# A graph-attention layer over sorted edges: 250 blocks of edges instead of 252

## The chip, the cores and the metric

The kernel runs on one core of one Trainium2 chip. The metric is the time of one launch on the device in microseconds (us). Several launches are timed and their median is given. One further launch was recorded by the hardware profiler, and everything that is read from a trace below comes from that single launch.

## The reference

There are N = 30000 nodes of 256 features and E = 510000 edges, one in each direction of 240000 random pairs and one loop for each node. The edges are sorted by their destination, and each has one of 8 types. The layer is

```
feat[r, n, h, :] = layernorm(x)[n] @ conv_weights[r, h]            # 8 types, 4 heads of 64
e[edge, h]  = leaky_relu(feat[type, src] . attn_l + feat[type, dst] . attn_r)
alpha       = softmax of e over the edges that share a destination
x           = x + sum over edges of alpha * feat[type, src] + h_bias
x           = x + (shared MLP + the two best of four expert MLPs)(layernorm(x))
```

A destination has about 17 edges. Which edges belong to which destination is only known from the data, so the kernel works it out on the chip.

## The kernel before

**Stage A** makes `feat` for all nodes. It runs over 235 tiles of 128 nodes. For each tile, TensorE makes five groups of columns (`group`, L304), ScalarE and VectorE bring them from PSUM into a tile `fo` (L306, L308), and SyncE stores the 1 MB of it to DRAM (`store`, L318). There are seven `fo` buffers. `erp_d` (what a destination contributes to the score) and `xb_d` (the input plus bias) are stored beside it.

While stage A runs, **side work** is slipped in. It is written as Python generators in a list `side`: `edge_records`, then `places`, then `expert_weights`. The function `aside` runs the first of them to its next `yield`. It is called once in a tile while `edge_records` is running, and twice in a tile afterwards (L699). So a `yield` more in `edge_records` puts off everything after it by one tile, and the order of instructions on each engine's queue is settled by that.

`edge_records` packs the edges into records, and then finds where the blocks begin. Edges are cut every `S` edges. Since a destination must not be split, block b begins at the first destination that begins at or after edge b*S. The block's first edge goes to `lo_sb`, its first node to `n_sb`. A block holds at most `CAP` = 2048 edges (16 for each of 128 partitions) and at most 128 nodes. The number of blocks is NBLK = ceil((E - CAP) / S), that is 252 with S = 2016, and one last block with 18 edges for each partition takes the end of the list. If a limit is broken, `bad` becomes 1, and a slow general path runs after the fast one (L1222 onward).

`places` runs over batches of 12 blocks: it loads their records (`fetch`, L519), prepares masks and indices on VectorE and GpSimd, and stores them to `rk_d` and `dk_d` (L590, L591). When all batches are done, two small tables go through TensorE and ScalarE to `thr_d` (L598, L601, L603).

`first_rows` starts when the tile counter m reaches `BT` + 2 = 178. For each block it gathers the `feat` rows of one edge for each partition (128 rows of 1040 bytes) with an indirect DMA on GpSimd (L632), and SyncE stores them to `stage` (L627). The gathers are spread evenly over the groups of the last 57 tiles.

**Stage B** runs over the blocks t = 0 .. NBLK. For a block, GpSimd gathers the other 15 rows for each partition with 15 indirect DMAs (`gather`, L962; the last block has 18), into a ring of four blocks. VectorE, ScalarE and TensorE make the scores, the softmax and the weighted sums (`dest_select`, `dest_pick`, `scores`, `weigh`, `onehot`, `sums`), each part emitted in one of six slots of a block. Blocks are put together in groups of four (`sizes`, L1127) for the MLPs: each group's 22 or so steps go into a list `todo`, and one step is taken in each slot.

The order of the work is written out by hand in both stages; no scheduler moves it.

Of the kernel before, what the change touches and what calls it, by code (L numbers as in the profile page):

```python
# [10 lines left out]
F32 = mybir.dt.float32  # L11
BF16 = mybir.dt.bfloat16
I32 = mybir.dt.int32
I16 = mybir.dt.int16
AF = mybir.ActivationFunctionType
ALU = mybir.AluOpType
AX = mybir.AxisListType
# [4 lines left out]
P = 128  # L22
# [9 lines left out]
EP = 120  # L32
EG = 85

U = 16
CAP = U * P
S = 2016
UL = 18  # L40
T = 4

# [3 lines left out]

WI, WD, WA, WP, W1 = 0, U, 2 * U, 3 * U, 5 * U
WT = W1 + 2 * (U + 1)
WR = WT + U * R // 2

# [6 lines left out]
def kernel(  # L57
# [26 lines left out]
    nc = tc.nc  # L84
    N = x.shape[0]
    E = src.shape[0]
# [4 lines left out]
    NGRP = EP * GPP  # L91
    NBLK = -(-(E - CAP) // S)
    NQ = NB
    assert EP * EG * GPP == E and 512 <= N < 32768 and NBLK * S + 64 <= E

    dram = ctx.enter_context(tc.tile_pool(name="dram", bufs=1, space=DRAM))
# [9 lines left out]
    thr_d = dram.tile([NBLK, 2, P], F32, name="thr_d")  # L106
    exc_d = dram.tile([P], F32, name="exc_d")
    KT = -(-(NBLK + 1) // P)
    lo_d = dram.tile([KT, P], F32, name="lo_d")
    n_d = dram.tile([KT, P], F32, name="n_d")  # L110
    uns_d = dram.tile([EP], F32, name="uns_d")
    mnmx = dram.tile([2, NGRP], F32, name="mnmx")
    lohi_d = dram.tile([NT, 2], I32, name="lohi_d")

# [19 lines left out]
    def layernorm(pool, xg, n, name, m=P):  # L134
# [10 lines left out]
        for t in range(n):  # L145
# [9 lines left out]
    w2 = wf.tile([P, 2, P], F32, name="w2")  # L155
# [15 lines left out]
                            pattern=[[1, NE], [-1, NE]], channel_multiplier=0)  # L171
# [10 lines left out]
                            pattern=[[1, P]], channel_multiplier=1)  # L182
# [38 lines left out]
    with ExitStack() as cx:  # L221
        wp = cx.enter_context(tc.tile_pool(name="wconv", bufs=1))
        xp = cx.enter_context(tc.tile_pool(name="xa", bufs=2))
        gp = cx.enter_context(tc.tile_pool(name="groups", bufs=1))
        cl = ExitStack()
# [119 lines left out]
        def edge_records(cl):  # L345
# [8 lines left out]
            n = gs * EG  # L354
            uns = gp.tile([EP, nch], F32, name="uns")
            ep = cl.enter_context(tc.tile_pool(name="edges", bufs=2))
            for c in range(nch):
# [8 lines left out]
                else:  # L366
                    nc.vector.memset(d_sb[:, 0:1], -1)
                    nc.sync.dma_start(d_sb[:, 1:], dstv[:, :n])
                    with nc.allow_non_contiguous_dma(reason="one edge of each partition, once"):
# [25 lines left out]
            zx = gp.tile([P, D], F32, name="zx")  # L395
# [6 lines left out]
                              zx.bitcast(BF16)[:, :R * 3 * H])  # L402
            yield


            WN = 64
            FAR = float(1 << 23)
            dw = gp.tile([P, KT, WN + 1], I32, name="dw")
            nc.gpsimd.memset(dw, -1)
            jj = gp.tile([P, WN], F32, name="jj")  # L410
            nc.gpsimd.iota(jj, pattern=[[1, WN]], base=0, channel_multiplier=0,
                           allow_small_or_imprecise_dtypes=True)
            first = gp.tile([P, KT], F32, name="first")
            irow = gp.tile([P, 1], F32, name="irow")
            nc.gpsimd.iota(irow, pattern=[[0, 1]], base=0, channel_multiplier=1,
                           allow_small_or_imprecise_dtypes=True)
            yield
            for k in range(KT):
                nc.vector.tensor_scalar(first[:, k:k + 1], irow, float(S), float(k * P * S), op0=ALU.mult,
                                        op1=ALU.add)  # L420
            nc.sync.dma_start(dw[0:1, 0, 1:], dst[0:WN].rearrange("(o c) -> o c", o=1))
            for k in range(KT):
                a = 1 if k == 0 else 0
                n = min(P, NBLK + 1 - k * P)
                nc.sync.dma_start(dw[a:n, k, :],
                                  bass.AP(tensor=dst.tensor, offset=dst.offset + (k * P + a) * S - 1,
                                          ap=[[S, n - a], [1, WN + 1]]))
            before_last = gp.tile([1, 1], I32, name="before_last")
            nc.sync.dma_start(before_last, dst[E - UL * P - 1:E - UL * P].rearrange("(o c) -> o c", o=1))
            yield  # L430
            lof = gp.tile([P, 2, KT], F32, name="lof")
            miss = gp.tile([P, KT, WN], F32, name="miss")
            nc.vector.tensor_tensor(miss, dw[:, :, 1:], dw[:, :, :WN], op=ALU.is_equal)
            yield
            for i, v in enumerate((jj[:, None, :].to_broadcast([P, KT, WN]), dw[:, :, 1:])):
                cand = gp.tile([P, KT, WN], F32, name="cand")
                nc.vector.scalar_tensor_tensor(cand, miss, FAR, v, op0=ALU.mult, op1=ALU.add)
                nc.vector.tensor_reduce(lof[:, i, :], cand, AX.X, ALU.min)
                yield
            nc.vector.tensor_add(lof[:, 0, :], lof[:, 0, :], first)  # L440
            nc.vector.tensor_scalar_min(lof[:, 0, :], lof[:, 0, :], float(E))
            nc.vector.tensor_scalar(lof[:, 1, :], lof[:, 1, :], 0.0, float(N), op0=ALU.max, op1=ALU.min)
            yield
            lor = gp.tile([1, KT * P], F32, name="lor")
            nr = gp.tile([1, KT * P], F32, name="nr")
            with nc.allow_non_contiguous_dma(reason="first edges and nodes of blocks, once"):
                for i, (t_d, row) in enumerate(((lo_d, lor), (n_d, nr))):
                    nc.sync.dma_start(t_d.rearrange("k p -> p k"), lof[:, i, :])
                    yield
                    if i:  # L450
                        nc.sync.dma_start(t_d[0:1, 0:1], zx[0:1, 0:1])
                        yield
                    nc.sync.dma_start(row, t_d.rearrange("(o k) p -> o (k p)", o=1))
                    yield
            nc.vector.tensor_copy(lo_sb, lor)
            nc.vector.tensor_copy(n_sb, nr)
            nc.vector.tensor_scalar_min(n0_sb, nr, float(N - P))
# [1 line left out]
            yield  # L459
            nc.vector.tensor_scalar(rowid[:, :NBLK], nbc, irow, None, op0=ALU.add)  # L460
            nc.vector.tensor_scalar_add(rowid[:, NBLK:], irow, float(N - P))
            unm = gp.tile([EP, 1], F32, name="unm")
            nc.vector.tensor_reduce(unm, uns, AX.X, ALU.max)
            yield
            with nc.allow_non_contiguous_dma(reason="one number of each partition, once"):
                nc.sync.dma_start(uns_d.rearrange("(p o) -> p o", o=1), unm)
            yield
            unr = gp.tile([1, EP], F32, name="unr")
            nc.sync.dma_start(unr, uns_d.rearrange("(o p) -> o p", o=1))


            two = gp.tile([1, 5], F32, name="two")
            gap = gp.tile([1, NBLK], F32, name="gap")
            for i, (row, most) in enumerate(((lor, CAP), (nr, P))):
                nc.vector.tensor_sub(gap, row[:, 1:NBLK + 1], row[:, :NBLK])
                nc.vector.tensor_reduce(two[:, i:i + 1], gap, AX.X, ALU.max)
# [4 lines left out]
            yield  # L481
            nc.vector.tensor_reduce(two[:, 4:5], unr, AX.X, ALU.max)
            nc.vector.tensor_reduce(bad, two, AX.X, ALU.max)

        BT = 3 * NT // 4
        count = {"ready": 0, "sent": 0}
# [3 lines left out]
        def places(cl):  # L490
# [3 lines left out]
            batches = [(b, min(GB, NBLK - b)) for b in range(0, NBLK, GB)]  # L494
            UW = U + 1
            no = gp.tile([1, 16], I16, name="no")
            nc.gpsimd.memset(no, -1)
            nc.sync.dma_start(dk_d[NBLK * CAP:].rearrange("(o c) -> o c", o=1), no)
            iu = gp.tile([P, U], F32, name="iu")
            nc.gpsimd.iota(iu, pattern=[[1, U]], base=0, channel_multiplier=0, allow_small_or_imprecise_dtypes=True)  # L500
# [142 lines left out]
        with tc.manual_schedule():  # L643
# [27 lines left out]
            while slot < 16:  # L671
                attention(slot, ab)
                slot += 1
            cl.close()
            side = [edge_records(cl), places(cl), expert_weights()]
            ahead = first_rows()

# [204 lines left out]
    with ExitStack() as cx:  # L882
# [242 lines left out]
        groups = {}  # L1125

        left, sizes = (NBLK + 1) % T, [T] * ((NBLK + 1) // T)  # L1127
        sizes = sizes[:-1] + [T - 1, 2] if left == 1 else sizes + [left] if left else sizes[:-1] + [2, 2]
        member = [(sum(sizes[:q]), n) for q, n in enumerate(sizes) for _ in range(n)]
        todo = []  # L1130
        late = []
# [91 lines left out]
    with tc.tile_pool(name="gr2", bufs=1) as gp, tc.tile_pool(name="ed2", bufs=2) as ep:  # L1223
        with tc.For_i(0, again):
# [4 lines left out]
            for g0 in range(0, GPP, gs):  # L1229
                c0, n = g0 * EG, gs * EG  # L1230
# [11 lines left out]
            base = gp.tile([P, ntg], F32, name="base")  # L1242
# [32 lines left out]
            for g in range(ntg):  # L1275
                n = min(P, NT - g * P)
# [3 lines left out]
    with ExitStack() as cx:  # L1280
# [13 lines left out]
        irow = cp.tile([P, 1], F32, name="irow")  # L1294
# [159 lines left out]
```

## Time and profile before

| | |
|---|---|
| median of 3 runs | 8487.05 us (8483.83 to 8509.22) |
| the profiled execution | 6603.28 us, of it the span 6601.5 us |
| mean granted TensorE clock in the span | 0.971 |
| stage A, first instruction to last matmul | 0 to about 1730 us |
| first gather of stage B, last one | 1750.3 us, 6513.1 us |
| busy, share of the span | PE 92%, DVE 80%, POOL 62%, ACT 52% |
| indirect gathers | 252 in stage A, 3798 in stage B |

PE is TensorE, DVE is VectorE, ACT is ScalarE, POOL is GpSimd, SPq is the queue of SyncE. The profiled execution is 22% shorter than the timed runs. The trace shows nothing of the difference, so it can be read only as to which engine waits for which, and by how much in that execution. The page gives, for each group of instructions, the number of them, their busy time, the mean duration of one, and the idle time of the engine ahead of them with what ended it. A window row gives a stretch of time, its length, the busy time (and count) of PE, PEld, DVE, ACT and POOL in it, the granted clock, the mean busy share of the 16 DMA engines and the GB/s they moved.

### The profile page before, as it was taken

To read this page: it belongs to the slowest core of one execution; us is meant where nothing else is said; L and a number is where in the kernel's file an instruction comes from. 1 tells how busy PE (TensorE), PEld (TensorE's weight loads), DVE (VectorE), ACT (ScalarE), POOL (GpSimd) and SP (SyncE) were. 2 spreads that over 40 slices of the span, in tenths; PEclk is the share of its full clock that TensorE was granted. 3 is DMA by queue.
4 is the path that set the end of the run, shared out by engine and by line. 5 is a ranking of instruction groups with operands and counts; after the bars stand their busy time and mean duration, and the time that the engine had idled before them with its cause. 6 is when DMAs were issued, how large, how long until landed. Compare 5 with 4: busy or idle time off the path is not lost. (4 is left out here: it accounts for less than half of the span.)

```text
span 6601.5 us, 97367 instructions
## 1 busy us (share of the span) xinstructions
PE 6047.9 (92%) x25770; PEld 3891.0 (59%) x25771; DVE 5254.8 (80%) x13699; ACT 3405.3 (52%) x8758; POOL 4082.8 (62%) x4424
## 2 busy tenths in 40 slices
PE   9999999999689989989899998899899999988998
PEld 5555555555356666666666666666666666666665
DVE  5555767644488888898888898898888888888895
ACT  2222222222256566666666665666656666566664
POOL 1111111266677777777777777777777777777773
PEclk9999999999899999999999999999999999999998
DMA  6666676799855555555555555555555555555552
GB/s 228 226 210 200 226 238 225 247 337 330 267 160 163 161 164 163 163 163 160 165 163 163 160 164 165 163 160 161 164 162 167 158 163 164 163 165 159 163 163 74
DMA packets 764586, 1214.72 MB, mean 184 GB/s; under 512 B 242498, under 2 KB 602917, under 8 KB 733813
## 3 DMA queue, kind: packets, MB, share of 16 engines
q1 hardware_dynamic: 568581, 668.72, 31.4%
q0 software_dynamic: 194400, 539.40, 29.3%
q8 instruction: 209, 3.42, 0.2%
q14 instruction: 356, 2.92, 0.1%
q10 hardware_dynamic: 1040, 0.26, 0.0%
HBM read 821.54 MB, written 386.43 MB: 183 GB/s over the span
## 5 line engine op out<-in xcount | busy, mean ns | idle before, releaser
L962 POOL DMA_INDIRECT ft<-feat,rk x3798 | 3606.7, 950 | 1169.0 <-issue 390.3
L1122 PE MATMUL po<-ft,oh 128*128 128x260 f32 x8100 | 2189.0, 407 | 137.1 <-DVE ho L1147 128.6
L1122 PEld LDWEIGHTS po<-ft,oh 128*128 128x128 f32 x8100 | 1520.4, 201 | 433.8 <-issue 196.5
L304 PE MATMUL ps<-w,xT 128*128 128x448 f32 (+1 forms) x4700 | 1708.4, 519 | 2.0 <-DMA w<-_L_gnn_conv_weights_dram 2.0
L1115 DVE TENSOR_TENSOR ft<-ft,p 128x768 f32<-128x768 f32 x1518 | 1292.2, 852 | 90.0 <-ACT ft L1108 86.1
L1049 ACT ACTIVATE oh<-icol,rk 128x128 f32<-128x128 f32 x4032 | 1327.7, 389 | 0.0
L304 PEld LDWEIGHTS ps<-w,xT 128*128 128x128 f32 x4700 | 875.6, 190 | 689.1 <-issue 603.3
L306 ACT COPY fo<-ps 128x448 f32<-128x448 f32 (+1 forms) x711 | 378.0, 533 | 1062.5 <-PE ps L304 972.5
L1050 ACT ACTIVATE oh<-oh 128x384 f32<-128x384 f32 x1518 | 741.1, 488 | 48.1
L1026 PEld LDWEIGHTS <-ohT 128*128 128x128 bf16 x4050 | 378.2, 158 | 408.9 <-issue 332.6
L1039 DVE TENSOR_REDUCE e<-ere 128x16 f32<-128x384 f32 (+1 forms) x1012 | 561.3, 555 | 34.6
L1037 DVE TENSOR_TENSOR ere<-pe,rk 128x384 f32<-128x384 f32 x1008 | 550.8, 546 | 1.3 <-PE pe L1026 1.3
L1107 ACT ACTIVATE p<-e 128x64 f32<-128x64 f32 (+1 forms) x253 | 70.2, 277 | 839.2 <-DVE e L1061 808.1
L1026 PE MATMUL pe<-erp,ohT 128*128 128x96 bf16 x4050 | 438.8, 233 | 60.5 <-DVE ohT L1009 37.5
L818 PE MATMUL ph<-xT,v 128*128 128x512 f32 (+2 forms) x1024 | 490.3, 602 | 0.4 <-ACT a L819 0.4
L306 DVE COPY fo<-ps 128x448 f32<-128x448 f32 (+1 forms) x464 | 242.3, 527 | 200.4 <-PE ps L304 194.1
L293 DVE COPY xT<-ptr 128x256 f32<-128x256 f32 x229 | 97.0, 424 | 368.6 <-PE ptr L291 367.0
L632 POOL DMA_INDIRECT fr<-feat,lowc x252 | 239.7, 951 | 193.7 <-DMA stage<-fr 90.2
L1009 DVE TENSOR_SCALAR ohT<-dr,rowid 128x2064 bf16<-128x2064 int16 (+1 forms) x253 | 323.6, 1279 | 19.8 <-DMA stage<-fr 19.7
L273 POOL TENSOR_TENSOR xb<-xg,hb 128x1024 f32<-128x1024 f32 (+1 forms) x59 | 140.7, 2385 | 272.1 <-DMA xg<-in_x_dram 161.9
L993 PE MATMUL t<-ident,fb 128*8 128x128 f32 x506 | 104.3, 290 | 214.9 <-DVE fb L1072 214.7
L819 ACT ACTIVATE a<-ph,c 128x512 f32<-128x512 f32 (+2 forms) x256 | 173.6, 678 | 195.7 <-PE ph L818 195.7
(219 smaller groups left out, 6810.9 us busy)
## 6 DMA issues: line engine op xcount, KB each, us to landing
feat<-fo SPq DMA_DIRECT2D x234, 1040.0 KB
dr<-dk_d SPq DMA_DIRECT2D x252, 516.0 KB
ft<-feat,rk POOLq DMA_INDIRECT x3798
stage<-fr SPq DMA_DIRECT2D x84, 390.0 KB
ft<-stage SPq DMA_DIRECT2D x252, 130.0 KB
xt<-xb_d SPq DMA_DIRECT2D x253, 128.0 KB
out_dram<-og SPq DMA_DIRECT2D x253, 128.0 KB
xb_d<-xb SPq DMA_DIRECT2D x58, 512.0 KB
```

The lines of the kernel that those rows point to most:

```text
L304: nc.tensor.matmul(ps, t["xT"][:, k, :], w[:, k, c0:c1], start=k == 0, stop=k == 1)
L306: eng(t["fo"][:, h0:h1, :HD], ps[:, :n].rearrange("p (a d) -> p a d", d=HD))
L818: nc.tensor.matmul(ps[:, :self.w], lhs, rhs, start=i == 0, stop=i == len(pairs) - 1)
L962: nc.gpsimd.indirect_dma_start(out=s.ft[:, u].rearrange("p h d -> p (h d)"), out_offset=None, in_=feat[:, :], in_offset=bass.IndirectOffse ...
L1009: nc.vector.tensor_scalar(ohT[:, :3 * s.dw].rearrange("n (i e) -> n i e", i=3), s.dr[:, :, :s.dw], rowid[:, t:t + 1], None, op0=ALU.is_equal)
L1026: nc.tensor.matmul(pe[:, u - u0].rearrange("p f r -> p (f r)"), s.ov[:, u, :], s.erp.rearrange("n h k r -> n (h k r)"), start=True, stop=True)
L1037: nc.vector.tensor_mul(ere, s.pe[:, :u1 - u0], s.th[:, u0:u1, None, :].to_broadcast([P, u1 - u0, H * 3, R]))
L1039: nc.vector.tensor_reduce(s.e[:, :, u0:u1].rearrange("p h u -> p u h"), ere.rearrange("p u (h k) r -> p u h (k r)", h=H), AX.X, ALU.add)
L1049: nc.scalar.activation(s.oh[:, u, :], icol, AF.Abs, bias=s.nd[:, u:u + 1])
L1050: nc.scalar.activation(s.oh[:, u0:u1], s.oh[:, u0:u1], AF.Relu, bias=1.0, scale=-1.0)
L1115: nc.vector.tensor_mul(fc, fc, pc[:, :, None].to_broadcast([P, (u1 - u0) * H, HD]))
L1122: nc.tensor.matmul(s.po.rearrange("n h d -> n (h d)"), s.oh[:, u, :], s.ft[:, u].rearrange("p h d -> p (h d)"), start=u == 0, stop=u == s. ...
```

## The change

`S` becomes 2032, so NBLK becomes ceil(507952 / 2032) = 250. The room for a border to slide falls from 32 edges to 16. Therefore each border now has two candidates: the destination that begins last before edge b*S, and the one that begins first at or after it. For each block it is worked out whether it keeps both limits if it begins early (`may[:, 0]`) and if it begins late (`may[:, 1]`), with its end at the late candidate. One scan over the borders then settles which candidate each takes: `late[b+1] = max(late[b] + may1 - 1, may0)`. The first edges and nodes are mixed from the candidates by `late`.

The window of edges looked at doubles from 64 to 128 for each border, four candidate rows go through DRAM (`cand_d`) into one partition instead of two rows, and the result `n_d` is stored from there. The small tiles of this part move from the pool `gp`, which lives for all of stage A, to a pool `bounds` that takes the place of the closed `edges` pool and is closed at the end of `edge_records`; `places` opens its own pool after it. The last lines let the MLP groups be cut for 251 blocks: one group of 2 in front, 61 of 4, then 3 and 2.

```diff
-S = 2016
+S = 2032
@@ edge_records
+            bp = cl.enter_context(tc.tile_pool(name="bounds", bufs=1))
-            dw = gp.tile([P, KT, WN + 1], I32, name="dw")
+            dw = bp.tile([P, KT, 2 * WN + 1], I32, name="dw")
...
-            for i, v in enumerate((jj[:, None, :].to_broadcast([P, KT, WN]), dw[:, :, 1:])):
-                cand = gp.tile([P, KT, WN], F32, name="cand")
-                nc.vector.scalar_tensor_tensor(cand, miss, FAR, v, op0=ALU.mult, op1=ALU.add)
-                nc.vector.tensor_reduce(lof[:, i, :], cand, AX.X, ALU.min)
-                yield
+            for i, v in enumerate((jj[:, None, :].to_broadcast([P, KT, 2 * WN]), dw[:, :, 1:])):
+                for f, (far, op) in enumerate(((-FAR, ALU.max), (FAR, ALU.min))):
+                    w2 = slice(f * WN, (f + 1) * WN)
+                    cand = bp.tile([P, KT, WN], F32, name="cand")
+                    nc.vector.scalar_tensor_tensor(cand, miss[:, :, w2], far, v[:, :, w2], op0=ALU.mult, op1=ALU.add)
+                    nc.vector.tensor_reduce(lof[:, i, f, :], cand, AX.X, op)
+                    yield
...
-                for i, (t_d, row) in enumerate(((lo_d, lor), (n_d, nr))):
-                    nc.sync.dma_start(t_d.rearrange("k p -> p k"), lof[:, i, :])
-                    yield
-                    if i:
-                        nc.sync.dma_start(t_d[0:1, 0:1], zx[0:1, 0:1])
-                        yield
-                    nc.sync.dma_start(row, t_d.rearrange("(o k) p -> o (k p)", o=1))
-                    yield
+                for k in range(4):
+                    nc.sync.dma_start(cand_d[k].rearrange("k p -> p k"), lof[:, k // 2, k % 2, :])
+                    yield
+                yield
+                nc.sync.dma_start(cands.rearrange("o i k -> o (i k)"),
+                                  cand_d.rearrange("(o i) k p -> o (i k p)", o=1))
+                yield
+                yield
+            nc.vector.memset(cands[:, 2:, 0:1], 0.0)
+            may = bp.tile([1, 2, NBLK], F32, name="may")
+            for f in range(2):
+                for i, most in enumerate((CAP, P)):
+                    gap = bp.tile([1, NBLK], F32, name="gap")
+                    nc.vector.tensor_sub(gap, cands[:, 2 * i + 1, 1:NBLK + 1], cands[:, 2 * i + f, :NBLK])
+                    if i == 0:
+                        nc.vector.tensor_scalar(may[:, f], gap, float(most), None, op0=ALU.is_le)
+                    else:
+                        nc.vector.scalar_tensor_tensor(may[:, f], gap, float(most), may[:, f], op0=ALU.is_le,
+                                                       op1=ALU.mult)
+                yield
+            nc.vector.tensor_scalar_add(may[:, 1], may[:, 1], -1.0)
+            late = bp.tile([1, KT * P], F32, name="late")
+            nc.vector.memset(late, 1.0)
+            nc.vector.tensor_tensor_scan(late[:, 1:NBLK + 1], may[:, 1], may[:, 0], 1.0, ALU.add, ALU.max)
+            yield
+            for i, row in enumerate((lor, nr)):
+                nc.vector.tensor_sub(row, cands[:, 2 * i + 1], cands[:, 2 * i])
+                nc.vector.tensor_mul(row, row, late)
+                nc.vector.tensor_add(row, row, cands[:, 2 * i])
+                yield
+            nc.sync.dma_start(n_d.rearrange("(o k) p -> o (k p)", o=1), nr)
+            yield
...
             nc.vector.tensor_reduce(bad, two, AX.X, ALU.max)
+            yield
+            cl.close()
@@ groups of blocks
-        sizes = sizes[:-1] + [T - 1, 2] if left == 1 else sizes + [left] if left else sizes[:-1] + [2, 2]
+        sizes = ([2] + sizes[:-1] + [3, 2] if left == 3 else sizes[:-1] + [T - 1, 2] if left == 1
+                 else sizes + [left] if left else sizes[:-1] + [2, 2])
```

## The prediction

> **What bounds the kernel now.** I read the page's busy shares first, then windows of the long stage, then GpSimd's instructions in order of time, then the end of stage A. The chain that ended last covers only 7 us near the end (the last matmuls `pf` and the sum `og`), so the bound has to be found in another way. The busy shares point to TensorE:
>
> ```profile
> PE 6047.9 (92%) x25770; PEld 3891.0 (59%) x25771; DVE 5254.8 (80%) x13699; ACT 3405.3 (52%) x8758; POOL 4082.8 (62%) x4424
> L962 POOL DMA_INDIRECT ft<-feat,rk x3798 | 3606.7, 950 | 1169.0 <-issue 390.3 <-PE po L1122 321.2 <-PE pe L1026 79.6
> ```
>
> Windows of stage B say otherwise. The columns are stretch, length, then PE, PEld, DVE, ACT and POOL, clock, DMA share, GB/s:
>
> ```profile
> 3000.00:4000.00 1000.00, 902.56 (x4325) 616.50 (x4325) 888.61 (x2291) 621.37 (x1639) 757.17 (x798) 0.97 0.57 162
> 4000.00:5000.00 1000.00, 904.74 (x4315) 617.22 (x4313) 887.83 (x2278) 621.08 (x1638) 757.13 (x798) 0.97 0.57 163
> 5000.00:6000.00 1000.00, 903.77 (x4332) 617.64 (x4332) 891.55 (x2291) 616.89 (x1633) 757.13 (x798) 0.97 0.57 163
> ```
>
> PE and DVE are each about 90% busy and their counts wander; POOL has exactly 798 gathers in each millisecond. GpSimd's own timeline (start, duration, instruction, idle ahead of it) shows why:
>
> ```profile
> 1737.36 0.94 POOL L632 DMA_INDIRECT fr<-feat,lowc  x1 [0.30 <-issue]
> 1750.34 0.94 POOL L962 DMA_INDIRECT ft<-feat,rk  x1 [12.04 <-DMA erp<-erp_d]
> 1751.59 0.95 POOL L962 DMA_INDIRECT ft<-feat,rk  x1 [0.30 <-issue]
> ...
> 6511.85 0.95 POOL L962 DMA_INDIRECT ft<-feat,rk  x1 [0.31 <-issue]
> 6513.10 0.95 POOL L962 DMA_INDIRECT ft<-feat,rk  x1 [0.30 <-issue]
> ```
>
> Every gather starts about 1.25 us after the one before, from the first to the last. The idle time of 0.30 us is the same whatever is named as its cause, so those "releasers" mean nothing: the gap is the pitch of the queue, and GpSimd, 62% "busy", never waits for the ring. From 1750.3 to 6514.1 it issues 3798 gathers: 4763.7 / 3798 = 1.254 us each, 15 x 1.254 = 18.8 us for a block. In the profiled execution stage B is bound by GpSimd.
>
> The end of stage A is bound by something else. PE runs without a gap to 1730 us, yet stage B begins 20 us later. DVE's last eviction of a tile (L308) beside SyncE's store of that tile (L318), for the tiles 4, 24 and 47 after 1305.8 us:
>
> ```profile
> 1335.05 0.20 DVE L308 COPY fo<-ps 128x32 f32<-128x32 f32 x1
> 1481.32 0.20 DVE L308 COPY fo<-ps 128x32 f32<-128x32 f32 x1
> 1649.41 0.20 DVE L308 COPY fo<-ps 128x32 f32<-128x32 f32 x1
> ```
> ```profile
> 1335.49 0.60 SPq L318 DMA_DIRECT2D feat<-fo  x1
> 1491.60 0.42 SPq L318 DMA_DIRECT2D feat<-fo  x1
> 1671.96 0.42 SPq L318 DMA_DIRECT2D feat<-fo  x1
> ```
>
> The store is 0.4 us late, then 10.3, then 22.6. The DMA engines are the cause:
>
> ```profile
> 1420.00:1440.00 20.00, 20.00 (x62) 10.88 (x61) 7.07 (x23) 4.71 (x10) 11.36 (x13) 1.00 1.01 355
> ```
>
> Since `first_rows` began (first gather 1308.8 us) they have been 87 to 104% busy, so the backlog grows by 22 us in 314. SyncE waits 248 us in all there for `fr` gathers to land.
>
> **What the Trainium skill says.** "DMA: Bandwidth & Descriptors", section "SWDGE vs HWDGE vs iDMA": for a DMA issued from GpSimd a core computes each descriptor pair in software. "Perfetto Trace Analysis", section "DMA Instruction — SWDGE (GPSIMD)": the profiled end is that of descriptor generation, not of the data. Both agree with a fixed 0.95 us for each gather while the DMA engines are only 57% busy. The first page, section "Issuing engines are not separate DMA queues": all issuers share the same 16 engines. The trace agrees: stores issued from SyncE fall behind when GpSimd's gathers start.
>
> **The change part by part**, summed against the profiled execution (6603.28 us: span 6601.5, and 1.8 around it).
>
> Two blocks fewer in stage B: 2 x 15 = 30 gathers x 1.254 = **-37.6 us**. The work of PE, DVE and ACT for these blocks goes too, but lies beside the gathers. The MLP groups stay 64 (before 62 of 4, then 3 and 2; after 2, 61 of 4, 3 and 2); the first small group brings 20 steps for the 24 slots until the next one ends, so no list builds up. The end is cut alike (4, 3, 2): the 87 us from the last gather to the end stay.
>
> In stage A, `first_rows` loses 2 gathers and stores of 130 KB each: 4 x 133 KB at about 340 GB/s = **-1.6 us** of saturated DMA.
>
> Bounds: some 23 more DVE instructions. A 1x252 difference took 0.40 us (L475), a 128-partition step on `cand` 0.28, a scan over 204 elements 0.76 at most: about 9 us in all. Two more small writes on SyncE at 0.5 us (L448), one store of `n_d`, one load less. All lies before 660 us, where PE is busy 400.00 of every 400 us and DVE 281 of 400, so I price it at nothing. Without that cover it would be 10 us. The waits are spaced: `cands` is needed 14.6 us after its load is issued, `lor` had 7.3 us before and DVE did not wait. The wait for `lor`'s write kept SyncE 4.9 us; a store of `feat` behind it has seven `fo` buffers, 51 us, to spare. The pool `bounds` makes the first `fetch` wait for DVE's last reduction, one tile earlier in the order. That SyncE wait, a few us, is likewise inside the buffers.
>
> What moves: `edge_records` goes from 19 yields after the records to 30. These are 11 tiles x 7.31 us = 80 us by which all of `places` and `expert_weights` comes later. Before, the last three batches were stored at 1222, 1243 and 1278 us and `thr_d` at 1281 and 1289, when the DMA engines were 79 to 86% busy (windows of 40 us). After, they come at about 1302, 1323, 1358, 1361 and 1369: two batches and the tables fall into the saturated stretch. In the packet records a batch's 1536 packets of 712 bytes took 43 ns each and 1536 of 32 bytes 14 to 18, over 16 engines 4.1 + 1.5 us; `thr_d` about 1. Together 2 x 5.6 + 1 = 12.2 us, less 1.6 gives 10.6 if none finds an idle DMA engine, -1.6 if all does. As the backlog grows steadily, nearly all should reach the end: I take +8. `expert_weights` moves inside the saturated stretch, from 1325 to 1405: nothing.
>
> Second, ScalarE: its copy L601 of the second table waits until the first has landed in DRAM, 7.07 us before, when DMA was free. Now the store is queued behind `stage` stores that wait for gathers, and behind the backlog, so 12 to 20 us. Evictions of three of five groups in each tile stand behind it, and PE has six PSUM buffers, some 7 us. PE may lose 0 to 13 us near 1370 us, of which the DMA backlog, 4 us then, covers some. I take +2.
>
> GpSimd: the last batches' copies of `places` now share its queue with `first_rows` (about 4 us in a batch of 4.5 tiles, beside 5.6 us of gathers in each tile of 7.3). It falls behind by a few us, and catches up by 1700.
>
> Sum: 6603.3 - 37.6 + 8 + 2 = 6575.7 us, -0.42%. The range by the bounds alone runs from -39 to -14 us.
>
> The timed median is 1.285 times the profiled time, and the profile does not say where the extra 1884 us lie. Scaled evenly: 8487.05 x 6575.7 / 6603.28 = **8451.6 us**. If they are constant: 8487.05 - 27.6 = 8459. If they lie in the gathers of stage B, a gather takes 1884 / 3798 = 0.50 us more, and 30 x 1.75 - 10 = 42.5 gives 8444.5.
>
> **The rivals.** *PE sets the pace in the timed runs.* PE at 90% beside a bound at 100% needs only a clock a tenth lower, and 1884 us would follow from a clock near 0.7. Then a block costs about 18.8 x 1.285 = 24 us, a tile of stage A takes longer, DMA is no longer full and the moved work costs nothing: 8487 - 48 = 8439. Against it stands the clock of 0.97 in the trace. *The gain is given back in stage A.* SyncE's lag also delays the loads of `x`: DVE already waits up to 5.1 us for `xg` near the end. If 12 us more of lag make DVE and then PE stall in each group of four tiles, stage B starts 20 to 25 us later, and 15 us are left, 8468. *Slower.* The place is the queue of ScalarE and PE at 1360 to 1375 us: copy L601 waits for a store behind SyncE's waits for gathers, PE stands, `feat` stores come late, gathers on them too. It decides at 38 us of stall, five times the wait of before; say 8505. For it speaks that GpSimd, SyncE, ScalarE and PE then hold each other in order; against it, that SyncE's single waits for gathers were 7.9 us at most. *The change does not do what it says.* Were a limit broken, the general path would add milliseconds. I worked the borders out from the inputs: with late borders alone 5 blocks have over 2048 edges (2052 at most); with the choice the most is 2048, and 126 nodes, and the last border is node 29882, past N - 128. So `bad` stays 0.
>
> **How the numbers follow.** The forecast 0.60, PE's pace 0.16, given back 0.15, slower 0.09. A difference within 0.3% (25 us) is about what measurement cannot tell from none. The first two are faster, 0.76; the third is the same, 0.15; slower 0.09. The range is 8426 to 8484: below PE's case for noise of the medians (25 us between the three runs), above the give-back; it leaves out the slower rival and a tenth of the rest. The forecast's own range is 8438 to 8464.
>
> **What would show it.** After: 3768 gathers at L962 at the same 1.25 us, none in wait; the first at 1755 to 1768 us; 87 us from last to end; last `rk_d` store near 1358. Wrong if the pitch changes, if POOL waits for the ring, if PE shows gaps before 1300 us, or if the first gather of stage B comes after 1785.

## The result and the profile after

| | before | after |
|---|---|---|
| median | 8503.72 us (16 runs, 8483.83 to 8527.46) | 8467.47 us (16 runs, 8446.90 to 8492.19) |
| ratio after / before | | 0.9962, interval 0.9950 to 0.9974 |
| profiled execution, its span | 6601.5 us | 8474.6 us |
| mean granted TensorE clock | 0.971 | 0.869 |

The change makes the kernel faster by 0.38%, about 32 us of 8504. The forecast was a ratio of 8451.6 / 8487.05 = 0.9958. The execution that was profiled before took 22% less than every timed run of that kernel; the one profiled after agrees with the timed runs. So the two spans can't be compared, and the first experiment profiles the kernel before once more.

Page of the kernel after, the busy shares and the gathers of stage B (busy us, mean ns, then the idle time ahead and what ended most of it):

```profile
PE 6526.9 (77%) x25626; PEld 4132.7 (49%) x25627; DVE 5265.9 (62%) x13646; ACT 3385.9 (40%) x8706; POOL 4053.6 (48%) x4392
L997 POOL DMA_INDIRECT ft<-feat,rk x3768 | 3576.7, 949 | 3013.0 <-PE po L1157 1589.6
```

The count of gathers is 3768, as forecast, and each still takes 0.95 us. But GpSimd now waits: 1589.6 us of its idle time end with the sums of an older block (`po`, L1157), that is, with a place in the ring of four blocks that comes free. In the first profile the largest entry was 390.3 us put down to "issue".

Windows of stage B of the kernel after (stretch, length, PE, PEld, DVE, ACT, POOL, clock, DMA share, GB/s):

```profile
3000.00:4000.00 1000.00, 725.68 (x3081) 481.32 (x3080) 644.17 (x1638) 443.22 (x1168) 541.76 (x572) 0.83 0.40 117
4000.00:5000.00 1000.00, 726.46 (x3105) 481.68 (x3103) 645.33 (x1645) 447.03 (x1181) 545.93 (x576) 0.85 0.40 117
```

There are 572 gathers in a millisecond where the first profile had 798, and no engine is above 73%. Lines of GpSimd's timeline show where stage B begins, and what a wait is like:

```profile
1756.82 0.95 POOL L667 DMA_INDIRECT fr<-feat,lowc  x1 [2.05 <-DMA stage<-fr]
1766.67 0.95 POOL L997 DMA_INDIRECT ft<-feat,rk  x1 [8.91 <-DMA stage<-fr]
...
4999.49 0.94 POOL L997 DMA_INDIRECT ft<-feat,rk  x1 [0.30 <-issue]
5019.84 0.95 POOL L997 DMA_INDIRECT ft<-feat,rk  x1 [19.41 <-PE po L1157]
```

Stage B begins at 1766.7 us, and in it GpSimd can stand for 19 us at a time. From the first gather to the last (8346.5 us) a block of 15 gathers takes 15 x 6579.8 / 3767 = 26.2 us, against 18.8 in the first profile.

Another worry of the forecast, ScalarE's wait for the table, is there, at 24.35 us and at the place named:

```profile
1384.06 0.37 ACT L636 COPY thr<-ps 122x256 f32<-122x256 f32 x1 [24.35 <-DMA thr_d<-thr]
```

PE lost 15.1 us behind it. The windows around it, of the kernel after:

```profile
1360.00:1380.00 20.00, 9.42 (x31) 5.01 (x29) 2.19 (x7) 0.00 (x0) 11.64 (x11) 0.79 0.95 282
1380.00:1400.00 20.00, 15.52 (x40) 8.22 (x41) 6.92 (x21) 5.65 (x13) 9.42 (x9) 0.78 1.00 246
```

### The profile page after: what moved, and what is told of

Its sections match the earlier page's. It is cut to its first block, busy times and chain, and to the rows that moved or that the text cites. A ratio compares the mean times of both kernels' runs of the same rounds, so it can differ in the third digit from the quotient of the medians.

```text
span 8474.6 us, 96817 instructions
## 1 busy us (share of the span) xinstructions
PE 6526.9 (77%) x25626; PEld 4132.7 (49%) x25627; DVE 5265.9 (62%) x13646; ACT 3385.9 (40%) x8706; POOL 4053.6 (48%) x4392
## 5 line engine op out<-in xcount | busy, mean ns | idle before, releaser
L997 POOL DMA_INDIRECT ft<-feat,rk x3768 | 3576.7, 949 | 3013.0 <-PE po L1157 1589.6
L1157 PE MATMUL po<-ft,oh 128*128 128x260 f32 x8036 | 2389.6, 438 | 310.2 <-DVE ho L1183 91.9
L1157 PEld LDWEIGHTS po<-ft,oh 128*128 128x128 f32 x8036 | 1637.5, 217 | 676.7 <-issue 388.9
L305 PE MATMUL ps<-w,xT 128*128 128x448 f32 (+1 forms) x4700 | 1709.4, 519 | 16.4 <-ACT thr L636 15.1
L1142 ACT ACTIVATE p<-e 128x64 f32<-128x64 f32 x251 | 69.6, 277 | 1304.1 <-DVE e L1096 1208.1
L1074 DVE TENSOR_REDUCE e<-ere 128x16 f32<-128x384 f32 x1004 | 557.0, 555 | 34.6
L799 ACT COPY xT<-ph 128x512 f32<-128x512 f32 (+1 forms) x128 | 73.2, 572 | 1097.0 <-remote 762.4
L853 PE MATMUL ph<-xT,w 128*128 128x512 f32 (+1 forms) x512 | 353.4, 818 | 203.4 <-issue 147.1
L906 PE MATMUL pf<-w,h 128*128 128x256 f32 x502 | 208.4, 505 | 355.8 <-ACT wT L899 193.0
L1044 DVE TENSOR_SCALAR ohT<-dr,rowid 128x2064 bf16<-128x2064 int16 x251 | 321.2, 1280 | 17.7 <-DMA stage<-fr 16.3
L1133 DVE TENSOR_TENSOR c<-t,rk 128x128 f32<-128x128 f32 x250 | 71.9, 288 | 407.6 <-remote 294.8
L908 PE MATMUL pf<-v,a 128*128 128x256 f32 x1004 | 316.8, 447 | 7.3 <-issue 5.4
```

The lines of the kernel that those rows point to most:

```text
L305: nc.tensor.matmul(ps, t["xT"][:, k, :], w[:, k, c0:c1], start=k == 0, stop=k == 1)
L853: nc.tensor.matmul(ps[:, :self.w], lhs, rhs, start=i == 0, stop=i == len(pairs) - 1)
L997: nc.gpsimd.indirect_dma_start(out=s.ft[:, u].rearrange("p h d -> p (h d)"), out_offset=None, in_=feat[:, :], in_offset=bass.IndirectOffse ...
L1044: nc.vector.tensor_scalar(ohT[:, :3 * s.dw].rearrange("n (i e) -> n i e", i=3), s.dr[:, :, :s.dw], rowid[:, t:t + 1], None, op0=ALU.is_equal)
L1074: nc.vector.tensor_reduce(s.e[:, :, u0:u1].rearrange("p h u -> p u h"), ere.rearrange("p u (h k) r -> p u h (k r)", h=H), AX.X, ALU.add)
L1157: nc.tensor.matmul(s.po.rearrange("n h d -> n (h d)"), s.oh[:, u, :], s.ft[:, u].rearrange("p h d -> p (h d)"), start=u == 0, stop=u == s. ...
```

## The experiments

Three questions are open: which pace stage B has in the runs that are timed; what the two blocks and the border code cost apart; and whether the give-back in stage A comes from ScalarE's wait or from the moved transfers. The table has the times read from the traces; the sections below use it. "Per block" is 15 mean pitches of the gathers.

| run | stage B begins | last gather | per block | last gather to end | last `rk_d` store | median, us | ratio to before |
|---|---|---|---|---|---|---|---|
| before, first profile | 1750.3 | 6513.1 | 18.8 | 88 | 1278 | | |
| e1_before_again | 1755.9 | 8391.9 | 26.2 | 125 | 1278 | 8518.7 | |
| after | 1766.7 | 8346.5 | 26.2 | 128 | 1368 | 8467.5 | 0.9962 (0.9950 to 0.9974) |
| e2_borders_only | 1777.9 | 8417.3 | 26.2 | 125 | 1377 | 8543.3 | 1.0034 (1.0024 to 1.0044) |
| e3_blocks_only | 1749.7 | 8318.6 | 26.2 | 127 | 1277 | 8455.2 | 0.9939 (0.9919 to 0.9958) |
| e4_two_thr | 1768.8 | 8358.3 | 26.2 | 131 | 1371 | 8487.7 | 0.9967 (0.9952 to 0.9981) |
| e5_early_side | 1743.1 | 8311.1 | 26.2 | 134 | 1072 | 8448.5 | 0.9940 (0.9921 to 0.9958) |
| e9_before_early | 1761.7 | 8432.8 | 26.4 | 126 | 1034 | 8558.4 | 1.0010 (0.9996 to 1.0024) |
| e10_early_again | 1750.6 | 8379.0 | 26.4 | 130 | 1074 | 8487.4 | 0.9935 (0.9919 to 0.9951) |

The kernels ran on several chips (on three of them the kernel before had 8501.6, 8511.5 and 8548.4), so only ratios are compared across them. e5 and e10 are one kernel: its stage B began at 1743.1 and at 1750.6, so a difference of less than about 8 us in that column says nothing by itself.

### The kernel before once more

No edit.

> The kernel before, unchanged, profiled once more. Theory A (the timed runs have another pace than the profile that the prediction read): its span is near 8500 us, a block of stage B takes about 26.2 us as it does in the profile after, GpSimd waits for the ring, and the first gather of stage B comes near 1750 us. Theory B (the extra 1884 us are a constant around the same execution): the span is again near 6600 us with 18.8 us for a block.

The second execution took 8518.71 us. Page and window of stage B of this run:

```profile
L962 POOL DMA_INDIRECT ft<-feat,rk x3798 | 3605.2, 949 | 3043.2 <-PE po L1122 1483.2 <-issue 784.3 <-remote 262.3
```
```profile
3000.00:4000.00 1000.00, 732.13 (x3090) 482.92 (x3090) 644.51 (x1642) 446.12 (x1180) 540.54 (x570) 0.84 0.41 116
```

These are the lines of the kernel after, not those of the first profile. Stage A is the same in both executions of the kernel before (stage B begins at 1750.3 and 1755.9), and most of the extra lies in stage B: 7.4 us x 253 blocks = 1870 of the 1915 us between the two spans. The same program therefore ran at two paces, and the profile that the forecast was read from shows the one that is not timed. That the bound of stage B is GpSimd's pitch falls for the timed runs.

### The borders alone, and the blocks alone

```diff
 # e2, against after
-S = 2032
+S = 2016
```
```diff
 # e3, against before; the edges past a block's capacity are left out
-S = 2016
+S = 2032
-        sizes = sizes[:-1] + [T - 1, 2] if left == 1 else ...
+        sizes = ([2] + sizes[:-1] + [3, 2] if left == 3 else sizes[:-1] + [T - 1, 2] if left == 1 ...
+            nc.vector.memset(bad, 0)
```

> The new borders with S = 2016, so 252 blocks as before: the price of the border code and of what it moves, alone. Theory A: stage B unchanged, its start 16 us later as in the profile after (ScalarE's copy of thr waits about 24 us): +16 us, ratio 1.002. Theory B, with the sizes of the prediction: +10 to +13 us. If the price is hidden: 0.

> The old borders with S = 2032 and 250 blocks, MLP groups as in the change; bad is set to 0, and in 5 blocks up to 4 edges over the limit are left out. The gain of two blocks alone. Theory A: 2 x 26.2 = -52 us, ratio 0.9938. Theory B (GpSimd's pitch of 1.254 us): -38 us, ratio 0.9956.

GpSimd's first gather of stage B, in e2 and then in e3:

```profile
1777.93 0.94 POOL L997 DMA_INDIRECT ft<-feat,rk  x1 [11.80 <-DMA erp<-erp_d]
```
```profile
1749.65 0.94 POOL L963 DMA_INDIRECT ft<-feat,rk  x1 [8.02 <-DMA stage<-fr]
```

The two blocks alone are worth 0.0061 x 8504 = 52 us (36 to 69), which is 2 x 26.2. The border code alone costs 0.0034 x 8504 = 29 us (20 to 37), more than the 16 expected of it; 22.0 of them stand in the trace as a later start of stage B (e1 to e2). The sum, -52 + 29 = -23, is beside the -32 (22 to 43) of the whole change within what these intervals allow. Both terms were forecast too small: -37.6, or -48 after scaling, and +10.

### A second buffer for the table

```diff
 # e4, against after
-            thr = gp.tile(..., name="thr")
+            thr = gp.tile(..., name="thr", bufs=2)
```

> The changed kernel with two buffers for thr, so that ScalarE's second copy doesn't wait for the first store to land. If that wait makes the loss in stage A: PE does not stand near 1365 us, and of the 16 us some 10 to 15 come back: -46 to -51 us against before, ratio 0.994 to 0.9946. If the late start of stage B is the DMA backlog alone, at most 3 us come back: -39 us, ratio 0.9954.

Windows of e4, the same stretch in which the kernel after lost 15 us:

```profile
1300.00:1400.00 100.00, 100.00 (x308) 54.54 (x307) 58.45 (x166) 26.42 (x57) 48.94 (x65) 1.00 1.01 288
1400.00:1500.00 100.00, 91.53 (x267) 48.99 (x266) 38.34 (x128) 21.57 (x48) 61.95 (x60) 0.97 1.00 341
```

ScalarE no longer waits, and PE is busy 100.00 of 100 us there. Nothing is gained in the end: PE loses 8.5 us in the next stretch, stage B begins at 1768.8 instead of 1766.7, and the ratio is 0.9967 instead of 0.9962. The wait of 24 us was real, and was not what made stage B late. What stays is a DMA share of 1.00 and the stores of `feat` behind it: SyncE's store of a tile comes 21 us after the last eviction of the tile near 1362 us, where the kernel after had 7 and e1 had 5 (means of the eight tiles from there). The longer stretch, in e1, after, e4 and e5 (the run of the next section), shows where the loss went:

```profile
1300.00:1700.00 400.00, 396.30 (x1194) 214.97 (x1193) 181.41 (x557) 100.76 (x217) 240.46 (x235) 1.00 0.95 327
1300.00:1700.00 400.00, 382.54 (x1147) 206.73 (x1146) 187.99 (x560) 96.01 (x209) 238.83 (x250) 0.98 0.97 324
1300.00:1700.00 400.00, 384.66 (x1150) 207.15 (x1148) 185.27 (x563) 94.60 (x210) 237.90 (x250) 0.99 0.99 325
1300.00:1700.00 400.00, 400.00 (x1206) 217.45 (x1205) 184.78 (x562) 102.82 (x218) 248.06 (x241) 1.00 0.94 327
```

PE loses 3.7 us there in e1, 17.5 in the kernel after, 15.3 in e4, 24.0 in e2 and none in e5, which goes with the starts of stage B in the table. The second buffer only moves the loss.

### The side work before the full stretch

```diff
 # e5, against after
-                    if g == 2 or g == 4 and len(side) < 3:
+                    if g == 2 or g == 4:
```

> The changed kernel, with the side work taken twice in a tile from its start, so that the records of edges and the borders take 40 tiles instead of 81 and places is stored some 290 us earlier, before the DMA engines are full. If the price of the change is the DMA work moved into the full stretch: the first gather of stage B comes at 1742 to 1750 us instead of 1767, and the kernel is about 22 us faster than the change, -54 to -60 us against before, ratio 0.993 to 0.9937. If the price is the border code itself (its waits on SyncE and VectorE): it stays, ratio 0.996.

The side work is now run twice in each tile from the start, so `places` is done at 1072 us instead of 1368, and the table's stores find idle DMA engines. First gather of stage B of e5, and its window beside that of the kernel after:

```profile
1743.10 0.94 POOL L997 DMA_INDIRECT ft<-feat,rk  x1 [9.15 <-DMA stage<-fr]
```
```profile
1040.00:1080.00 40.00, 40.00 (x126) 21.87 (x125) 24.58 (x67) 10.49 (x25) 7.64 (x14) 1.00 0.72 232
1300.00:1400.00 100.00, 100.00 (x303) 54.41 (x302) 45.14 (x142) 25.55 (x54) 55.88 (x54) 1.00 0.89 309
```
```profile
1300.00:1400.00 100.00, 84.94 (x254) 45.90 (x253) 49.05 (x137) 21.72 (x48) 53.43 (x68) 0.91 0.98 289
```

The last batches now run at a DMA share of 0.72 with PE at 40.00 of 40, and between 1300 and 1400 the DMA engines have a tenth of their time left. Stage B begins 23.6 us earlier than after. The ratio is 0.9940: this kernel beats both.

### Early side work, with the change and without

Is e5 faster because it undoes the change's lateness, or because early side work is good in any case?

```diff
 # e9, against before; e10 is e5 again
-                    if g == 2 or g == 4 and len(side) < 3:
+                    if g == 2 or g == 4:
```

> The kernel before, with 252 blocks and one candidate for each border; only the side work is run twice in every tile from the start, as in e5_early_side. If e5 gains because places no longer falls into the stretch of full DMA, this kernel has little to win: there places was nearly done before that stretch (last store of rk_d at 1278 us, first_rows from 1305), so stage B begins 0 to 13 us earlier than in e1_before_again, and the ratio to before is 0.9985 to 1.0. If running the side work early is worth the same whatever the borders, it wins what e5 won over after, 19 to 24 us, ratio about 0.9975, and the change itself is then worth no more than in after.

> The same kernel as e5_early_side, beside e9_before_early on the same chip. It differs from e9 only by the change. If the change's cost is only the lateness of places, then with early side work in both the two blocks are worth their whole 52 us less the few that the border code takes, 40 to 50 us, and the ratio to before is about 0.994, as e5 had it. If the border code has a cost of its own, the difference between the two is about 30 us, as between after and before.

Without the change, early side work brings nothing (1.0010, interval 0.9996 to 1.0024). Stage B even begins 5.8 us later than in e1, where 0 to 13 us earlier was expected: early side work has a price of its own, since PE loses 8.2 us between 60 and 660 us in e9 and 4.0 in e10, and none in e1. With it, it brings the whole gain again (0.9935).

From e9 to e10, which differ by the change alone, the ratio is 0.9925, with the two intervals put together 0.990 to 0.995, or -64 us (46 to 82); the two profiled spans differ by 50. So the border code has no price of its own that these runs can see (some 18 us to each side): its 23 instructions more on VectorE are hidden, as forecast. Its price in the kernel after is that it put `places` into the full stretch. Which part of `places` costs the time there was not tried apart. The windows point to the DMA engines (share 0.98 from 1300 to 1400 us) and not to GpSimd, which also has work of those batches (busy 53.43 of 100 us), but no run moves the stores alone. Against e5 and e10 together (0.9938), the kernel after gives back 21 us, with an interval of about 15 to each side.

### What sets the pace of stage B

```diff
 # e6: half of the gathers (7 of 15) are left out, from cleared buffers
-            for u in range(1 if s.own else 0, s.u):
+            for u in range(1 if s.own else 0, s.u // 2):
 # e7: half of the sums are left out (stop moves to u == s.u - 2)
-            for u in range(s.sc[c], s.sc[c + 1]):
+            for u in [v for v in range(s.sc[c], s.sc[c + 1]) if v % 2 == 0]:
 # e8: the MLPs are left out
-                todo.extend(groups.pop(q).steps())
+                groups.pop(q)
+                for i in range(n):
+                    put(q + i, x1[:, i, :])
 # e11: each selection of dest_expand is made twice, with the same outcome
-            for u in range(u0, u1):
+            for u in [v for v in range(u0, u1) for _ in range(2)]:
```

> The changed kernel with 7 instead of 15 gathers for a block (the other rows stay as a memset left them, so the sums are of other numbers). If GpSimd's pitch sets the pace of stage B, as the prediction read it: 8 x 1.254 = 10 us less for each block, the span falls by 2500 us or to the next bound. If the pace is set on TensorE and the engines that wait for it: about 26 us for a block as before, span within 100 us of 8475.

> The changed kernel with every second matmul of the weighted sums left out (the sums are over half of the edges): 16 records of 0.22 us less on TensorE in each block, 3.5 us. If TensorE's work sets the pace: 22 to 23 us for a block, span about 7600 us. If GpSimd does: no change. If the pace is a chain of waits that the MLP steps begin: less than 2 us for a block.

> The changed kernel without the MLP steps (the rows after the attention are stored as they are): TensorE loses about 7 us of work for a block, and the long waits of ScalarE for xT and of VectorE near the steps go. If the MLP's steps make the pace of 26.2 us: the pitch falls to GpSimd's 18.8 us, span about 6600 us. If something else does (the loads on SyncE, the semaphores): it stays over 22 us.

> The changed kernel, in which TensorE makes each of the 16 selections of a block (matmul into pe, 227 ns each with its weights) twice in a row, so that it has 16 x 0.23 = 3.6 us more work in a block and the same outputs. It asks whether the pace of 26.2 us comes from TensorE being idle. Theory: gaps in TensorE's work lower its granted clock (0.83 in stage B), the lower clock lengthens the gaps, and more work in the gaps keeps the clock up: then the clock of stage B rises to 0.95 or more, a block takes 19 to 22 us and the kernel 6700 to 7400 us. Rival: TensorE's work is part of the chain that sets the pace: then a block takes 1 to 3.6 us longer and the kernel 8700 to 9350 us. Third: the pace comes from elsewhere and the work fits into the gaps: 8467 within 30 us, with the clock near 0.87.

Windows of stage B, of e6, e7, e8 and e11 in turn:

```profile
3000.00:4000.00 1000.00, 856.10 (x3892) 586.21 (x3892) 803.53 (x2064) 560.32 (x1471) 317.59 (x335) 0.91 0.32 95
```
```profile
3000.00:4000.00 1000.00, 688.23 (x2530) 408.92 (x2531) 653.46 (x1670) 457.38 (x1199) 561.25 (x592) 0.71 0.41 120
```
```profile
3000.00:4000.00 1000.00, 590.41 (x2495) 445.51 (x2493) 686.16 (x1644) 369.63 (x1104) 635.96 (x670) 0.76 0.47 137
```
```profile
3000.00:4000.00 1000.00, 741.37 (x3732) 514.70 (x3732) 647.80 (x1647) 447.37 (x1176) 534.39 (x565) 0.86 0.40 116
```

| run | taken away from a block | us per block | change against after | time, us |
|---|---|---|---|---|
| e6_half_gathers | 8 gathers, 10.0 us of GpSimd by their pitch | 20.6 | -5.6 | 7092.0 |
| e7_half_sums | 8 of 16 sums, 3.5 us of PE by their pitch | 25.5 | -0.7 | 8308.1 |
| e8_no_mlp | all of the MLPs | 22.5 | -3.7 | 7477.3 |
| e11_more_pe | nothing; 16 selections more, 1.0 us of PE | 26.1 | -0.1 | 8443.7 |

e6, e7 and e8 are one execution each, e11 two. e11 added less than was expected of it. The record of a selection lasts 227 ns, but the next one starts 63 ns after it, so the records overlap. The time for which the selections keep TensorE busy, after and then in e11 (stretch, length, PE, and VectorE on the same tile, then clock, DMA share, GB/s):

```profile
3000.00:4000.00 1000.00, 67.86 (x608) 83.99 (x153) 0.83 0.40 117
3000.00:4000.00 1000.00, 108.21 (x1232) 84.67 (x154) 0.86 0.40 116
```

608 selections are those of 38 blocks, 1232 those of 38.5. TensorE's time for them went from 1.8 to 2.8 us in a block, so 1.0 us was added and not 3.6.

TensorE's work does not show as the bound: 8 sums less bring 0.7 us, and the 1.0 us more costs nothing. The first of these is weakened by the clock, which fell to 0.71, so that TensorE's whole busy time in a block went only from 19.0 to 17.6 us. Nor does GpSimd's pitch alone set the pace: a block of e6 needs 7 x 1.25 = 8.8 us of it and takes 20.6, which is neither the 10 us less nor the unchanged 26 that were expected. The gathers and the MLPs both have a part. The 0.7 us of e7 was expected for a chain of waits that the MLP steps begin, but e8, without these steps, stays at 22.5 us and not at GpSimd's 18.8, so that chain is not all of it. Between the two paces of the kernel, 18.8 and 26.2 us, TensorE's busy time in a block differs by 2 us only (17.0 and 19.0, from the windows at 3000 us); the rest of the 7.4 is time in which no matmul is on record.

e11 was also to test an idea from the Trainium skill, "TensorE: Matmul & The Clock Gate", section "HAM oscillation — how this bites in real kernels": gaps of more than about 3.4 us in TensorE's work lower its clock. Between 3000 and 6000 us the kernel after has 81 such gaps (565 us in all), the first profile of the kernel before 10 (40 us), and the clock is 0.83 to 0.85 against 0.97, as that page would have it. But e7 has 85 (561 us), about as many as the kernel after, and 0.71, so the number of such gaps alone does not give the clock here. In e11 they went down to 55 (497 us), the clock rose from 0.83 to 0.86, and a block still took 26.1 us. With 1.0 us of work this is a weak test. Whether the clock is a cause of the slower pace or goes with it is not settled.

What a slow stretch looks like, in the timeline of the kernel after:

```profile
5033.12 0.36 PE L1127 MATMUL t<-ident,turn 8*128 8x4 f32 x2
...
5054.58 0.29 DVE L1133 TENSOR_TENSOR c<-t,rk 128x128 f32<-128x128 f32 x1 [20.70 <-remote]
5055.99 0.59 ACT L799 COPY xT<-ph 128x512 f32<-128x512 f32 x1 [15.54 <-remote]
```

VectorE needs the two small products `t`, which by the record end at 5033.5, and starts 21 us later (`remote`: the trace names no instruction that ended the wait); ScalarE waits in the same way for `ph`, recorded before 5034.1. Over the run, VectorE's `c` starts 6.2 us after the recorded end of `t` in the mean, and more than 8 us after it in 105 of 251 blocks. In the first profile of before it was 1.0 us, and never more than 2.4. The Trainium skill, "Perfetto Trace Analysis", section "Tensor Engine Instruction (MATMUL, LD_WEIGHTS)", says that a matmul's recorded end is an estimate; the lag agrees with that, but no run here shows what TensorE does in those 20 us. In e11 the long lags of `t` are down to 24 blocks while the pace stays, so they are not the whole story.

## Why the prediction was right, and where it wasn't

**The sum.** Direction and size were right: -0.42% forecast, -0.38% measured. That the size came out is in part luck. The two terms behind it were both too small, and their errors offset each other: -52 + 20 (after against e3; about 19 to each side) or -52 + 29 (e2), where the forecast had -37.6 + 10 in the first profile's time, that is -48 + 13 after scaling. In absolute time, 8467.5 lies 16 us above the forecast 8451.6 and beside the 8468 of the rival *given back in stage A*. But both were subtracted from 8487.05, the median of 3 runs, and 16 runs of the same kernel gave 8503.7, so the ratio is what can be compared.

**"In the profiled execution stage B is bound by GpSimd"**, 1.254 us for a gather: true of that execution, and it is the term that was mis-sized for the timed runs. There a block takes 26.2 us, GpSimd waits for the ring 1589.6 us, and both stand against "none in wait" and "the same 1.25 us". The extra time lies nearly all in stage B (e1), so the case of a constant extra, 8459, falls. The last of the ways named, 0.50 us more for each gather, had the right price for the two blocks, 30 x 1.75 = 52.5 us against 52 measured, though a gather itself still takes 0.95 us and it is the waits between gathers that grew. The even scaling by 1.285 gave 24.2 us for a block and was near for a wrong reason: stage A was not scaled at all, so stage B was scaled by 1.39. The rival *PE sets the pace* named about 24 us and a lower clock, and the clock did fall; but e7 speaks against TensorE's work as the bound (e11 added too little to say much), and stage A, against what that rival said, kept its clock (1.00 in e1 from 660 to 1400 us), its full DMA engines (0.96 to 0.98 from 1360 to 1400) and so its price.

**"Bounds: priced at nothing"** holds: e9 and e10. In the kernel after, the code runs from 412 to 636 us, and PE shows 400.00 of 400 us between 260 and 660; no time of PE is lost between 660 and 1300 either. The "281 of 400" given there for VectorE belongs to a later stretch (281.71 from 860 to 1260 us); from 260 to 660 it is 221.26, so the cover was wider than stated.

**"What moves: +8"** was the right mechanism, mis-sized. The last `rk_d` store came at 1368.5 us (forecast near 1358), the copy of the table waited 24.35 us (12 to 20), PE lost 15.1 us (0 to 13). Counting only the transfer time of the two batches, 12.2 us, left out that PE stalls as well when the stores fall behind; 20 to 29 us are given back. From e3 to the kernel after PE loses 15.0 us more between 1300 and 1700 us and stage B begins 17.0 us later; from e1 to e2 these are 20.3 and 22.0. The rival *given back in stage A* had 20 to 25 us for that, and saw the place where the loss would go. It said that 15 us would be left, since it set this against -37.6 and not against -52.

**"Second, ScalarE: +2"** was wrong in kind: the wait, and the stall of PE behind it, came, but cost nothing on top of the full DMA engines: in e4 both are gone at this place, PE loses about as much in the 300 us that follow, and the kernel ends no earlier. The same holds for the rival *slower*, which rests on that queue.

**"The first gather at 1755 to 1768 us"**: 1766.7. **"87 us from last gather to end"**: the level was that of the first profile; it is 125 in e1 and 128 after, so the change left it alone, as forecast.

**Open.** Why one execution of the kernel before ran at 18.8 us for a block and all others at about 26 is not settled. Removing gathers or the MLPs shortens the block, removing half of the sums hardly does; no run adds much work to TensorE, and none isolates the cause.

## What to carry to other kernels

Before a bound is read from a profile, compare its span with the timed runs: where they differ by a fifth, profile the same kernel again, or the bound may be that of an execution which nobody times. Code that is hidden on its engine can still cost by what it pushes back: eleven more steps of side work for the borders cost nothing themselves that the runs can see, but made two batches and a table meet a stretch in which the DMA engines were full, and took back some 20 of 52 us. Such work belongs ahead of that stretch (one condition changed here, ratio 0.994), while removing the one visible wait inside it (24 us on ScalarE) moved the loss and gained nothing.

## What the runs showed of the hardware

- One program took 6601.5 us in one execution and 8517.0 in another, with stage A alike within 6 us and each block of stage B 7.4 us longer.
- A consumer can start up to 22.9 us after the recorded end of the matmul that it needs (mean 6.2 us after, 1.0 in the first profile).
- Halving the sums made the granted clock of stage B fall from 0.83 to 0.71, and the block only 0.7 us shorter; halving the gathers raised it to 0.91.
- The record of a selection (a bf16 matmul, 128 x 96) lasts 227 ns, while the next one starts 63 ns later: 16 more of them in a block kept TensorE busy 1.0 us longer, not 3.6, and cost nothing measurable in a block of 26.2 us (ratio to before 0.9927, interval 0.9898 to 0.9956).
- 81 gaps of over 3.4 us in TensorE's work went with a clock of 0.84 (kernel after, 3000 to 6000 us), and 85 with 0.71 (e7).
